# Attention blocks of a gated transformer kernel: sums by adding transfers, tokens turned by squares, and a bank of its own for a22

## The chip, the core and the metric

The kernel runs on one core of a Trainium2 chip. The metric is device time in microseconds of one launch, the median of several runs. The engines are TensorE (PE), VectorE (DVE), ScalarE (ACT), GpSimd (POOL) and SyncE (SP); SP, ACT and POOL can each issue DMA transfers.

## What is computed

Eight batches of 512 tokens of 512 features pass four layers in float32. The change touches the first:

```python
def _L0_xattn_ref(query, kv, Wq, Wg, bg, Wkv, Wo):      # H = 16 heads of 32
    q = query @ Wq.T
    gate = sigmoid(query @ Wg.T + bg)
    k, v = split(kv @ Wkv.T, 2, axis=-1)
    q, k = feature_map(q), feature_map(k)               # where(x > 0, x + 1, exp(x)), per head
    kv_summary = einsum("bhsd,bhse->bhde", k, v)
    z = 1.0 / (einsum("bhld,bhd->bhl", q, k.sum(axis=-2))[..., None] + 1e-6)
    attn = einsum("bhld,bhde->bhle", q, kv_summary) * z
    return attn * gate @ Wo.T

x = x + tanh(g_xattn[0]) * _L0_xattn_ref(layernorm(x), ctx, ...)
x = x + tanh(g_ffn[0]) * feed_forward(layernorm(x))          # 512 -> 2048 -> 512, gelu
x = x + tanh(g_xattn[1]) * masked_softmax_attention(layernorm(x), ctx)
x = x + tanh(g_ffn[1]) * grouped_experts(layernorm(x))       # routed, 8 groups
```

## The kernel before

**Blocks and products.** The work goes batch by batch (a block is one batch). Each weight product is done as seven half-size products, with sums and differences of quarters (a11, a12, a21, a22 of the tokens, b of the weights) instead of eight products of quarters. One `step(m)` is one of these seven: eight matmuls of 128x256, then `after(m, p)`, which takes the result out of a PSUM bank. A unit (`QUp`, `GUp`, `ODown` in the attention) has banks x (products 1, 6, 7, 4), w (5, 3) and z (2). Products of one bank accumulate on each other, so a reader between them must finish before the next one of that bank starts. `steps` puts the last two products of a unit (its `order` behind `head`) after the first product of the next unit, so that they fill PE there.

**The attention loop** (`for b in range(B)`) does for block b: q (`QUp`), the numerators of block b - 1 (`numerators`, `attended`), g (`GUp`), then the output unit `ODown` of block b - 1, with the denominators of b between its steps. `denominators` writes 1/z for 16 heads, each repeated over eight rows, to a DRAM tile; `spread` reads it back so that each head's row stands on 32 partitions, and `gated` multiplies it into the gate in the next block's q steps. PE, DVE and ACT follow the scheduler's order there, except where the code puts them into `in_order`; SP and POOL issue in program order.

**The preparation of block b + 1** (`prep_xa0`, through `normed`) is a generator; `some(prep)` in the loop takes its next part. It takes statistics on DVE, normalizes on ACT, and turns the tokens into features by 16 PE transposes against the identity (four tiles, L524), each tile copied from PSUM by ACT (L526). Then `token_combinations` makes the four sums S of quarters on DVE. From the second block of the feed-forward on, the tokens are turned differently: DVE transposes squares of 32x32 (L562) and 16 DMA transfers bring the squares to their partitions (L581).

**The sums onto x.** x of a block stays in SBUF. `Down.after` adds each product, scaled by the gate, onto its quarter of x with DVE (L1048), seven times per block. After the last one x is stored to the DRAM tile `between["ff0", b]`, from which the feed-forward loads it later.

**Pools.** `t2` (`temp`) holds eight buffers of 128x512 that all copies out of PSUM, feature maps and z share in turn. PSUM has four banks `ps` (transposes, numerators, denominators) and four `acc` in the attention. `over` is the one buffer for the spread denominators. A builder (`tick`, `build_first`) loads and combines the feed-forward's weights beside all this, on DVE and SP.

Of the kernel before, what the change touches and what calls it, by code (L numbers as in the profile page):

```python
# [68 lines left out]
def flamingo_kernel(  # L69
# [46 lines left out]
    bank = {"ps": ps, "xn": awork}  # L116
# [66 lines left out]
    def store_x(ph, b):  # L183

        t = xs.pop((ph, b))
        if ph == "ff1":
            for i in range(NT):
                nc.sync.dma_start(out=out[ds(b * S + i * P, P), :], in_=t[:, i, :])
        else:

            nc.scalar.dma_start(out=between[{"xa0": "ff0", "ff0": "ff1"}[ph], b], in_=t)
# [35 lines left out]
    for h in range(P // HD):  # L227
        nc.vector.memset(heads[ts(h, HD), ts(h, 8)], 1.0)
    neg_half = const.tile([P, NT], F32, tag="neg_half", name="neg_half")
# [245 lines left out]
    def normed(ph, b, tag, normed_part=lambda t: None):  # L475

        xb = xs[ph, b]
        by_products = ph == "xa0" or tag == "ff0_0"
        xnT = work.tile([P, NC, S] if ph == "xa0" else [P, NC, NT, P], F32, tag="xnT", name=f"xnT_{tag}")
# [35 lines left out]
        if by_products:  # L515

            def normed_tile(t):
                xn[t] = bank["xn"].tile([P, D], F32, tag="xn", name=f"xn_{tag}_{t}", bufs=2)
                norm(t, xn[t])

            def turn(t):
                pt = psum(f"pt_{tag}_{t}").rearrange("p (c q) -> p c q", q=P)
                for c in range(NC):
                    nc.tensor.transpose(pt[:, c, :], xn[t][:, ts(c, P)], ident)  # L524
                if ph == "xa0":
                    nc.scalar.copy(xnT[:, :, ts(t, P)], pt)  # L526
                else:
                    nc.scalar.copy(
                        xnT[:, :, t].rearrange("p q (c i) -> p c q i", c=NC),
                        pt.rearrange("p c (q i) -> p c q i", q=NC),  # L530
                    )

            if ph == "xa0" and b == 0:
                normed_tile(0)
                normed_tile(1)
                yield
                for t in range(NT):
                    turn(t)
                    if t + 2 < NT:
                        normed_tile(t + 2)  # L540
                    yield
                return xnT
            if ahead:
                normed_tile(0)
                yield
            for t in range(NT):
                if not ahead:
                    normed_tile(t)
                elif t + 1 < NT:
                    normed_tile(t + 1)  # L550
                turn(t)
                normed_part(t)
                yield
            return xnT
# [3 lines left out]
        xn = bank["xn"].tile([P, NC, NT, P], F32, tag="xn", name=f"xn_{tag}")  # L558
# [18 lines left out]
        for q in range(NC):  # L577
            for l in range(NC):
                with here("gpsimd"):
                    queue = nc.sync if tag.startswith("ff1") else nc.gpsimd  # L580
                    queue.dma_start(out=xnT[ts(l, HD), q], in_=xn[ts(q, HD), l])  # L581
# [6 lines left out]
    def features_of(ph, xnT):  # L588

        if ph == "xa0":  # L590
            return xnT.rearrange("p c (t q i) -> p c t q i", q=NC, i=HD)
        return xnT.rearrange("p q t (c i) -> p c t q i", c=NC)
# [7 lines left out]
    def keys_values():  # L600
# [15 lines left out]
        def projected(what, pair):  # L616
            p = banks[what, pair] = psum(f"p{what}_{pair}")
            for c in range(NC):
                nc.tensor.matmul(
                    p, lhsT=ctxT[pair][:, c, :], rhs=w_kv[what, c], start=c == 0, stop=c == NC - 1  # L620
                )
# [58 lines left out]
    def token_combinations(ph, b, xnT):  # L680

        s = work.tile([P, 4, 2, H2], F32, tag="S", name=f"S_{ph}_{b}", bufs=1)
        if ph == "xa0":
            v = features_of(ph, xnT).rearrange("p c t q i -> p c t (q i)")
            a11, a12, a21, a22 = (v[:, ts(h, 2), ts(r, 2)] for r in range(2) for h in range(2))
            to = s.rearrange("p k c (t i) -> p k c t i", t=2)
        else:
            a11, a12, a21, a22 = (xnT[:, :, ts(r, 2), ts(h, 2 * HD)] for r in range(2) for h in range(2))
            to = s.rearrange("p k c (q t i) -> p k (c q) t i", q=2, t=2)
        nc.vector.tensor_tensor(to[:, 0], a21, a22, ALU.add)  # L690
        nc.vector.tensor_tensor(to[:, 1], to[:, 0], a11, ALU.subtract)
        nc.vector.tensor_tensor(to[:, 2], a11, a21, ALU.subtract)
        nc.vector.tensor_tensor(to[:, 3], a12, to[:, 1], ALU.subtract)
        if ph == "xa0":
            return to.rearrange("p k c t (q i) -> p k c t q i", i=HD)
        return to.rearrange("p k q t (c i) -> p k c t q i", c=2)
# [12 lines left out]
    def cross_attention(b):  # L709
# [23 lines left out]
        for c in range(NC):  # L733
            for r in range(2):
                nc.tensor.matmul(  # L735
                    pst[ts(r, M), :],
                    lhsT=ctxT[:, c, :],
                    rhs=features_of("ff1", xnT)[:, c].rearrange("p (u r) q i -> p r u q i", r=2)[:, r],
                    start=c == 0,
                    stop=c == NC - 1,  # L740
                )
# [46 lines left out]
    def prep_ff1(b):  # L788
# [4 lines left out]
        for c in range(NC):  # L793
            for t in range(NT):
                nc.tensor.matmul(
                    plt[ts(t, E), :],
                    lhsT=router_sb[:, c, :],
                    rhs=features_of("ff1", xnT)[:, c, t],
                    start=c == 0,
                    stop=c == NC - 1,  # L800
                )
# [69 lines left out]
    class Unit:  # L871
# [3 lines left out]
        order, head = ORDER, 5  # L875

        def step(self, m):
            name = BANK[m]
            if m in OPENS:
                self.banks[name], self.numbers[name] = acc_bank(f"{name}_{self.tag}")  # L880
            self.product(m, self.banks[name])
            self.after(m, self.banks[name])
            if m in CLOSES and self.numbers[name] is not None:
                idle_banks.append(self.numbers[name])
# [5 lines left out]
        def mark(self, m, k):  # L890

            return dict(start=m in OPENS and k == 0, stop=True, skip_group_check=True)

    class Up(Unit):
# [6 lines left out]
        def product(self, m, p):  # L901
            xnT, s = blocks[self.ph, self.b][0:2]
            v = features_of(self.ph, xnT)
# [113 lines left out]
    class Down(Unit):  # L1017
# [21 lines left out]
        def after(self, m, p):  # L1039

            xb = xs[self.ph, self.b]
            parts = {1: (1, 1), 2: (1, 1), 6: (1, 2), 7: (2, 2), 4: (2, 1), 3: (1, 2)}
            todo = [(parts[m], p)] if m in parts else []
            if m == 7:
                todo.append(((2, 2), self.banks["w"]))
            for (r, c), src in todo:
                dst = xb[:, ts(r - 1, 2), ts(c - 1, H2)]
                nc.vector.scalar_tensor_tensor(dst, src, GATE[self.ph], dst, ALU.mult, ALU.add)  # L1048
# [3 lines left out]
            if m == 3:  # L1052
                stores.append((self.ph, self.b))
# [193 lines left out]
    def denominators(b, q):  # L1247
# [7 lines left out]
        nc.vector.tensor_scalar(z, pd, ATT_EPS, None, ALU.add)  # L1255
        yield
        for r in range(2):
            nc.vector.reciprocal(z[:, ts(r, H2)], z[:, ts(r, H2)])
            yield
        over[b] = dram.tile([P, S], F32, tag=f"over{b}", name=f"over_{b}")  # L1260
        nc.sync.dma_start(out=over[b], in_=z)
        yield

    def spread(b):

        rows = over[b].rearrange("(c h k) t -> c k h t", c=NC, k=8)
        over[b] = aunits.tile([P, NC, S], F32, tag="over", name=f"spread_{b}")
        for h in [slice(0, 2), slice(2, 4)] if b == B - 1 else [slice(0, 4)]:
            for c in range(NC):
                nc.sync.dma_start(out=over[b][ts(c, HD), h], in_=rows[c, 0, h].partition_broadcast(HD))  # L1270
# [41 lines left out]
    class ODown(Down):  # L1312
        def __init__(self, b):
            super().__init__("xa0", b, 2)
            self.prefix = "x"

# [42 lines left out]
    projected("k", 0)  # L1359
    projected("k", 1)  # L1360
# [34 lines left out]
    set_aside()  # L1395
    first.close()
    bank["acc"] = phase.enter_context(tc.tile_pool(name="acc", bufs=4, space=PSUM, reuse_waits="tile"))
    aunits = phase.enter_context(tc.tile_pool(name="attention_units", bufs=1, reuse_waits="tile"))
    in_order -= {"tensor", "vector", "scalar"}
# [9 lines left out]
    for b in range(B):  # L1409
# [4 lines left out]
        for n, (u, m) in enumerate(steps([q])):  # L1414
# [5 lines left out]
            if n == 4:  # L1420
                flush()
                if b < B - 1:
                    some(prep)
            tick()
        if done:
# [3 lines left out]
        for n, (u, m) in enumerate(steps([g])):  # L1429
# [12 lines left out]
            if n == 3 or n > 3 and not done:  # L1442
# [10 lines left out]
        for n, (u, m) in enumerate(steps([ODown(done[0])] if done else [])):  # L1453
# [9 lines left out]
            if n in ((0, 1, 3, 5) if b < B - 1 else (6,)):  # L1463
                some(prep)
            tick()
        for _ in prep:
            pass
# [53 lines left out]
    for u, m in [*steps([ODown(B - 1)]), *late]:  # L1521
        u.step(m)
    late.clear()
# [12 lines left out]
    bank["xn"] = hpool  # L1536
# [11 lines left out]
    def groups():  # L1548
        nc.vector.tensor_copy(mg_f, mg_i)
        for g in range(G):  # L1550
            nc.vector.tensor_scalar(of_group[:, g, :], mg_f, float(g), None, ALU.is_equal)
# [10 lines left out]
    EARLY = (25,27,29,31,33)  # L1562
# [100 lines left out]
```

## Time and profile before

| what | value |
|---|---|
| median of three runs | 2017.96 us (2016.71 to 2019.13) |
| profiled execution, its own time | 2017.31 us |
| its span (first to last instruction) | 2015.5 us |
| busy: PE, DVE, ACT, POOL | 99%, 75%, 32%, 11% of the span |
| granted TensorE clock | 0.999 |
| DMA moved | 508.81 MB, 252 GB/s on average |

In the profile a line such as `L916 PE MATMUL x_q<-xnT_xa,w_q` gives the code line, engine, operation, and the tile written and the tiles read. Line L60 is a helper through which instructions in program order pass, so tiles tell more there than lines. The attention stage lies between about 45 and 378 us of the span; the keys and values stand before it, the feed-forward layers behind it.

### The profile page before, as it was taken

The page shows a single profiled execution, that of the slowest core. Times are in us where ns is not written, and L with a number is a line of the kernel's source. Part 1 is how long each engine was busy: PE and PEld are TensorE (multiplying, and loading weights), DVE is VectorE, ACT ScalarE, POOL GpSimd, SP SyncE. Part 2 cuts the span into 40 slices and gives each one's busy share as a digit, 9 for nine tenths or more (in the row PEclk, how much of TensorE's full clock was granted, in tenths as well). Part 3 has the DMA queues.
Part 4 walks back from the last instruction along what each step waited for, and adds up shares of the span by engine and source line. Part 5 has one row for each costly group of instructions (what it writes and reads, how often), then busy time and mean ns, then how long its engine had stood idle before and what let it go on. Part 6 is the DMA issues. An engine that isn't in the chain of part 4 may idle for free.

```text
span 2015.5 us, 35095 instructions
## 1 busy us (share of the span) xinstructions
PE 1999.7 (99%) x12428; PEld 1777.3 (88%) x12428; DVE 1509.6 (75%) x3012; ACT 648.4 (32%) x1294; POOL 220.6 (11%) x387
## 2 busy tenths in 40 slices
PE   9999999999999999999999999999999999999998
PEld 5888887899989899999989889898989888898988
DVE  4788888676857676767868687877778786877758
ACT  3543443323242424233344232313132232313121
POOL 3000000101010101011211120110202020110000
PEclk9999999999999999999999999999999999999999
DMA  7366555799999998999987969696978879696865
GB/s 210 131 214 185 185 162 165 228 324 290 317 292 301 301 299 282 305 297 292 316 265 259 313 213 316 191 309 194 307 228 248 278 231 300 195 317 182 280 202 172
DMA packets 318061, 508.81 MB, mean 252 GB/s; under 512 B 42944, under 2 KB 109664, under 8 KB 313792
## 3 DMA queue, kind: packets, MB, share of 16 engines
q1 hardware_dynamic: 302768, 464.05, 72.7%
q0 software_dynamic: 9264, 19.31, 3.4%
q10 hardware_dynamic: 5856, 23.20, 3.1%
q8 instruction: 101, 1.65, 0.3%
q14 instruction: 72, 0.59, 0.1%
HBM read 413.04 MB, written 69.27 MB: 239 GB/s over the span
## 4 chain that ended last, share of the span: by engine, by line
PE 94%; DVE 4%; ACT 1%; issue 1%; DMA 0%; POOL 0%; SPq 0%; DVEq 0%; ACTq 0%
PE x_ff L916 27%; PE w_ff L916 13%; PE x_ff_down L1111 13%; PE w_ff_down L1111 9%; PE z_ff L916 7%; PE v_ff_down L1111 4%; PE z_ff_down L1111 4%; PE x_xa_down L1032 2%; PE x_q L916 2%; PE x_g L916 2%; PE w_xa_down L1032 1%; PE w_g L916 1%; PE w_q L916 1%; PE pst L735 1%; PE pv L60 1%; PE z_q L916 1%
## 5 line engine op out<-in xcount | busy, mean ns | idle before, releaser
L916 PE MATMUL w_ff<-S_ff,w_ff 128*128 128x256 f32 x1280 | 303.8, 380 | 0.2 <-DVE up_ff L1009 0.2
L916 PE MATMUL x_ff<-S_ff,w_ff 128*128 128x256 f32 x1280 | 302.9, 379 | 1.0 <-ACT u_ff L928 1.0
L916 PE MATMUL x_ff<-xnT_ff,w_ff 128*128 128x256 f32 x1280 | 297.4, 380 | 0.0
L928 ACT COPY u_ff<-x_ff 128x512 f32<-128x512 f32 x240 | 140.1, 584 | 452.7 <-PE x_ff L916 418.0
L916 PEld LDWEIGHTS x_ff<-S_ff,w_ff 128*128 128x128 f32 x1280 | 242.3, 190 | 35.0 <-ACT u_ff L928 1.6
L916 PEld LDWEIGHTS w_ff<-S_ff,w_ff 128*128 128x128 f32 x1280 | 241.0, 190 | 36.0 <-issue 2.7
L916 PEld LDWEIGHTS x_ff<-xnT_ff,w_ff 128*128 128x128 f32 x1280 | 239.5, 190 | 33.3 <-issue 1.6
L1111 PE MATMUL x_ff_down<-w_ff_down,split_ff_down 128*128 128x128 f32 x1344 | 161.9, 275 | 0.0
L1111 PEld LDWEIGHTS x_ff_down<-w_ff_down,split_ff_down 128*128 128x128 f32 x1344 | 155.9, 192 | 0.0
L916 PE MATMUL z_ff<-xnT_ff,w_ff 128*128 128x256 f32 x640 | 152.9, 380 | 0.0
L1125 DVE TENSOR_TENSOR part_ff_down<-part_ff_down 128x128 f32<-128x128 f32 x315 | 84.3, 286 | 75.6 <-ACT part_ff_down L1138 65.7
L916 PEld LDWEIGHTS z_ff<-xnT_ff,w_ff 128*128 128x128 f32 x640 | 119.9, 190 | 20.7 <-issue 5.3
L495 POOL TENSOR_TENSOR rstd_ff<-var_ff,neg_half 128x4 f32<-128x4 f32 x15 | 15.5, 1033 | 866.6 <-DVE nshift_ff L494 866.6
L1111 PE MATMUL w_ff_down<-w_ff_down,split_ff_down 128*128 128x128 f32 x896 | 107.9, 275 | 0.0
L1111 PEld LDWEIGHTS w_ff_down<-w_ff_down,split_ff_down 128*128 128x128 f32 x896 | 103.9, 192 | 0.0
L1009 DVE TENSOR_TENSOR up_ff<-w_ff,u_ff 128x512 f32<-128x512 f32 x96 | 65.6, 684 | 27.1 <-ACT u_ff L928 27.1
L976 ACT ACTIVATE a_ff<-a_ff,b_sb 128x256 f32<-128x256 f32 x128 | 58.1, 501 | 84.9 <-DVE a_ff L971 84.9
L1111 PE MATMUL x_ff_down<-w_ff_down,a_ff 128*128 128x128 f32 x672 | 82.9, 275 | 0.0
L1111 PE MATMUL w_ff_down<-w_ff_down,s_ff 128*128 128x128 f32 x672 | 82.8, 275 | 0.0
L971 DVE TENSOR_TENSOR a_ff<-w_ff,u_ff 128x512 f32<-128x512 f32 x64 | 43.9, 685 | 52.0 <-ACT u_ff L928 51.5
L999 DVE SCALAR_TENSOR_TENSOR g_ff<-th_ff,x_ff 128x512 f32<-128x512 f32 x48 | 32.7, 680 | 65.1 <-ACT th_ff L998 65.1
L1111 PEld LDWEIGHTS w_ff_down<-w_ff_down,s_ff 128*128 128x128 f32 x672 | 80.0, 192 | 0.8
(267 smaller groups left out, 3456.4 us busy)
## 6 DMA issues: line engine op xcount, KB each, us to landing
w_ff_down<-stream_ff SPq DMA_DIRECT2D x680, 256.0 KB
w_ff<-ff_up SPq DMA_DIRECT2D x560, 256.0 KB
stream_ff<-build_ff_down SPq DMA_DIRECT2D x49, 448.0 KB
x_ff<-x_ff SPq DMA_DIRECT2D x16, 1024.0 KB
share<-shares SPq DMA_DIRECT2D x64, 256.0 KB
ff_up<-build_ff_up SPq DMA_DIRECT2D x42, 256.0 KB
x_ff<-x_xa ACTq DMA_DIRECT2D x8, 1024.0 KB
x_ff<-x_ff ACTq DMA_DIRECT2D x8, 1024.0 KB
```

The source lines that it names most:

```text
L60: made = f(*args, **kw)
L495: nc.gpsimd.tensor_tensor(rstd, var, neg_half, ALU.pow)
L735: nc.tensor.matmul(pst[ts(r, M), :], lhsT=ctxT[:, c, :], rhs=features_of("ff1", xnT)[:, c].rearrange("p (u r) q i -> p r u q i", r=2)[:, r ...
L916: nc.tensor.matmul(p[:, n, :], lhsT=w[:, c, ts(n, P)], rhs=moving, **self.mark(m, 2 * n + c),)
L928: nc.scalar.copy(self.s[m], p)
L971: nc.vector.tensor_tensor(h, p, s, ALU.add)
L976: nc.scalar.activation(h[:, n, :], p[:, n, :], AF.Gelu, bias=b1_sb[:, f : f + 1])
L999: nc.vector.scalar_tensor_tensor(g, th, 1.0, p, ALU.add, ALU.mult)
L1009: nc.vector.tensor_tensor(u, p, s, ALU.add)
L1032: nc.tensor.matmul(p[:, t, :], lhsT=a[:, k, ts(t, P)], rhs=w[k // 2][:, k % 2, :], **self.mark(m, 2 * k + t),)
L1111: nc.tensor.matmul(p[bank][:, place, :], lhsT=operand[k][:, c, :], rhs=w[at // 4][:, ts(at % 4, P)], start=bank not in opened, stop=True, ...
L1125: return lambda: nc.vector.tensor_tensor(m(k), m(k), m(by), ALU.add)
```

## The change

- The output unit's products are taken in the order 1, 2, 4, 6, 5, 7, 3, all seven before the next unit (`head` 7), and product 4 opens a PSUM bank y of its own, from the pool `ps`.
- In blocks 0 to 6 each sum onto x is made of a copy by ACT, scaled by the gate, into a `t2` buffer, and a transfer of the POOL queue that adds the buffer onto `between["ff0", b]` in DRAM. There are eight such sums per block. x itself is stored to that tile before them, in the loop's q steps. The last block (7) keeps DVE's sums.
- Blocks 2 to 7 are turned by squares with 16 transfers on SP; their normalized tokens lie in the buffer `over`. Blocks 0 and 1 keep the PE transposes, with the layout of the squares.
- The denominators of blocks 0 to 6: ACT adds epsilon, one transfer writes 16 rows to DRAM, a second brings them back as 128 x 64, DVE takes the reciprocal of that, a third writes it to `over`'s DRAM tile of 16 rows. All three are on the POOL queue.
- The parts of the preparation are taken at other steps. The keys of the first two context pairs are projected with their matmuls interleaved. `groups` keeps DVE in program order.

```diff
@@ store_x @@
-        t = xs.pop((ph, b))
+        t = xs[ph, b] if ph == "xa0" else xs.pop((ph, b))
...
@@ normed @@
-        by_products = ph == "xa0" or tag == "ff0_0"
-        xnT = work.tile([P, NC, S] if ph == "xa0" else [P, NC, NT, P], F32, tag="xnT", name=f"xnT_{tag}")
+        by_products = tag in ("xa0_0", "xa0_1", "ff0_0")
+        xnT = work.tile([P, NC, NT, P], F32, tag="xnT", name=f"xnT_{tag}")
...
-        xn = bank["xn"].tile([P, NC, NT, P], F32, tag="xn", name=f"xn_{tag}")
+        xn = bank["xn"].tile([P, NC, NT, P], F32, tag=bank["tag"], name=f"xn_{tag}")
...
-                    queue = nc.sync if tag.startswith("ff1") else nc.gpsimd
+                    queue = nc.sync if ph == "xa0" or tag.startswith("ff1") else nc.gpsimd
...
@@ projected @@
-        def projected(what, pair):
-            p = banks[what, pair] = psum(f"p{what}_{pair}")
+        def projected(what, *pairs):
+            for pair in pairs:
+                banks[what, pair] = psum(f"p{what}_{pair}")
             for c in range(NC):
-                nc.tensor.matmul(
-                    p, lhsT=ctxT[pair][:, c, :], rhs=w_kv[what, c], start=c == 0, stop=c == NC - 1
-                )
+                for pair in pairs:
+                    nc.tensor.matmul(
...
@@ Unit.step @@
-            name = BANK[m]
-            if m in OPENS:
-                self.banks[name], self.numbers[name] = acc_bank(f"{name}_{self.tag}")
+            name = self.bank_of[m]
+            if m in self.opens:
+                if name == "y":
+                    self.banks[name], self.numbers[name] = halves(psum(f"{name}_{self.tag}")), None
+                else:
+                    self.banks[name], self.numbers[name] = acc_bank(f"{name}_{self.tag}")
...
@@ Down.after @@
+            if 4 in self.opens and m == 5:
+                todo.append(((2, 2), p))
+            if 4 in self.opens and m == 7:
+                todo[1:] = [((2, 1), p)]
             for (r, c), src in todo:
-                dst = xb[:, ts(r - 1, 2), ts(c - 1, H2)]
-                nc.vector.scalar_tensor_tensor(dst, src, GATE[self.ph], dst, ALU.mult, ALU.add)
+                if self.b == B - 1:
+                    dst = xs[self.ph, self.b][:, ts(r - 1, 2), ts(c - 1, H2)]
+                    nc.vector.scalar_tensor_tensor(dst, src, GATE[self.ph], dst, ALU.mult, ALU.add)
+                    continue
+                t = halves(temp(f"sum{m}{r}{c}_{self.tag}"))
+                nc.scalar.activation(t, src, AF.Identity, scale=GATE[self.ph])
+                nc.gpsimd.dma_start(
+                    out=between["ff0", self.b][:, ts(r - 1, 2), ts(c - 1, H2)], in_=t, accum_op=ALU.add
+                )
...
@@ denominators @@
+        of_heads = z.rearrange("(n k) t -> n k t", k=8)[:, 0, :]
+        over[b] = dram.tile([P // 8, S], F32, tag=f"over{b}", name=f"over_{b}")
+        if b == B - 1:
...
+        nc.scalar.activation(z, pd, AF.Identity, bias=eps, scale=1.0)
+        under = dram.tile([P // 8, S], F32, tag=f"under{b}", name=f"under_{b}")
+        narrow = small.tile([P, S // 8], F32, tag="narrow", name=f"narrow_{b}")
+        with here("gpsimd"):
+            nc.gpsimd.dma_start(out=under, in_=of_heads)
+            nc.gpsimd.dma_start(out=narrow, in_=under.rearrange("n (u q) -> (n u) q", u=8))
+        yield
+        yield
+        nc.vector.reciprocal(narrow, narrow)
+        with here("gpsimd"):
+            nc.gpsimd.dma_start(out=over[b].rearrange("n (u q) -> (n u) q", u=8), in_=narrow)
...
@@ ODown @@
+            self.order, self.head = (1, 2, 4, 6, 5, 7, 3), 7
+            self.bank_of, self.opens = {**BANK, 4: "y"}, (*OPENS, 4)
...
@@ the attention loop @@
-    projected("k", 0)
-    projected("k", 1)
+    projected("k", 0, 1)
...
+    stores.append(("xa0", 0))
+    flush()
...
+    bank.update(xn=aunits, tag="over")
...
-            if n == 4:
-                flush()
-                if b < B - 1:
-                    some(prep)
+            if n == 4 and b + 1 < B - 1:
+                stores.append(("xa0", b + 1))
+            if n in ((4,) if b == 0 else (0, 3, 5) if b < B - 1 else ()):
+                some(prep)
             tick()
+        flush()
...
-            if n == 3 or n > 3 and not done:
+            if n in ((0, 2) if b < B - 1 else (3,)) or n > 2 and not done:
                 some(prep)
...
-            if n in ((0, 1, 3, 5) if b < B - 1 else (6,)):
+            if n in ((2,) if b < B - 1 else (6,)):
                 some(prep)
+            if n == 4 and b < B - 1:
+                for _ in prep:
+                    pass
             tick()
-        for _ in prep:
-            pass
+        while b < B - 1 or prep not in ready:
+            if next(prep, prep) in (prep, "last"):
+                ready.add(prep)
+                if b == B - 1:
+                    break
+                for _ in prep:
+                    pass
+                break
...
@@ behind the loop @@
-    for u, m in [*steps([ODown(B - 1)]), *late]:
+    for n, (u, m) in enumerate([*steps([ODown(B - 1)]), *late]):
         u.step(m)
+        if n == 4:
+            for _ in prep:
+                pass
```

## The prediction

> **What bounds the kernel now.** First the head of the page:
>
> ```profile
> span 2015.5 us, 35095 instructions
> ...
> PE 1999.7 (99%) x12428; PEld 1777.3 (88%) x12428; DVE 1509.6 (75%) x3012; ACT 648.4 (32%) x1294; POOL 220.6 (11%) x387
> ```
>
> TensorE is busy in 99% of the span, so only two things can move the time: PE work that disappears, and PE waits that come or go. The change lies in the attention stage (about 45 to 378 us), so next the busy time of one whole block there, from one block's numerators to the next:
>
> ```profile
> core 0: us, PE busy (x) PEld busy (x) DVE busy (x) ACT busy (x) POOL busy (x), PEclk, DMA share, GB/s
> 205.20:245.60 40.40, 40.40 (x225) 33.70 (x224) 32.45 (x54) 17.34 (x31) 1.70 (x2) 1.00 0.52 171
> ```
>
> PE has no gap in it, DVE is at 80%, ACT at 43%, the DMA engines at half. What PE does in it shows in its timeline (start, length, line):
>
> ```profile
> 221.27 0.66 PE L524 MATMUL pt_xa<-ident,xn_xa 128*128 128x128 f32 x4
> 221.76 1.89 PE L916 MATMUL x_g<-xnT_xa,w_g 128*128 128x256 f32 x8
> 223.49 0.60 PE L524 MATMUL pt_xa<-ident,xn_xa 128*128 128x128 f32 x4
> 223.93 1.89 PE L916 MATMUL w_g<-S_xa,w_g 128*128 128x256 f32 x8
> 225.66 1.89 PE L1032 MATMUL z_xa_down<-w_o,a 128*128 128x256 f32 x8
> 227.38 0.60 PE L524 MATMUL pt_xa<-ident,xn_xa 128*128 128x128 f32 x4
> 227.82 1.89 PE L1032 MATMUL x_xa_down<-w_o,s_xa 128*128 128x256 f32 x8
> ```
>
> The distance from start to start counts, not the length: a product of eight matmuls holds the queue 1.73 us (223.93 to 225.66), a turned tile 0.44 to 0.49 us. That is the price of a turn, because PE takes them in order and idles nowhere near them. Last, all that PE waits for:
>
> ```profile
> PE x_g L916 <- ACT u_g L928: 1.8, 3, 1.2
> PE pk L60 <- DMA w_k<-in_wkv: 1.1, 1, 1.1
> ...
> PE pd L60 <- DVE q L673: 1.1, 1, 1.1
> ...
> PE x_xa_down L1032 <- DVE x_xa L1048: 0.8, 1, 0.8
> ```
>
> With the rows of 0.7 and 0.6 us that follow, the attention's own waits (without the keys' 1.1) come to 5.0 us, and all of them have a late ACT or DVE behind them.
>
> **Part 1, the turns.** Blocks 2 to 7 lose four turned tiles each. In the block shown they cost 0.49 + 0.44 + 0.44 + 0.43 = 1.80 us, six blocks 10.8 us. All of it is on the path. The group's mean of 277 ns would give 96 x 0.277 = 27 us, but it counts overlapped ends; I take the pace. (The Trainium skill, "TensorE: Matmul & The Clock Gate", Part 4: PE-mode transpose, has about 275 ns for a transpose within one kernel, which is this mean; as a cost it would make the gain an estimated 26 us. No gap in this trace supports that.)
>
> In their place come four squares on DVE (the same instruction at L562: median 702 ns, 2.8 us a block) and 16 transfers of 64 KB, now on SP. SP issues the same transfers in the second feed-forward at 0.59 us (L581), so 9.4 us of SP per block, where SP spends some 22 of 43 us between 202 and 245 us. Squares end near the third step of g; the next block's first product is 13 steps, 22 us, later; 9.4 + 2 of landing need 11.5. Behind an ff_up store (7 issues, 13.1 us at 204.8) they would be 2 to 3 us late. There are four such stores: 0 to 10 us in all.
>
> **Part 2, the sums.** DVE loses seven L1048 per block (0.747 us: 5.2), two reciprocals of 256 columns (3.4) and the add of epsilon (0.7); with squares 2.8 and a reciprocal of 64 columns (a quarter of 1.73: 0.4) it falls by 6.1 to about 26 of 38.6 us. ACT gains eight gated copies and one z at about 0.59 (L928 reads a bank so) and loses four turn copies (0.58): plus 3, to 20 of 38.6. Neither becomes the bound. The bank waits get looser: a sum's reader has at least one other product (1.73 us) before its bank is written again, also because a22 has a bank of its own. Of the 5 us of old waits I take half as gone: 2.5 (none to all).
>
> Each copy needs a buffer of the eight of t2 until its adding transfer has read it. Step by step the buffer's next user comes six products or more later, 10 us. No adding transfer is in the trace. Bounds: below, a plain 64 KB transfer of the POOL queue; above, twice the bytes.
>
> ```profile
> xnT_xa<-xn_xa POOLq DMA_DIRECT2D x128, 64.0 KB, 6.4
> ...
> xnT_ff<-xn_ff POOLq DMA_DIRECT2D x112, 64.0 KB, 5.1
> ...
> ctxd<-in_ctx POOLq DMA_DIRECT2D x16, 128.0 KB, 4.0
> ```
>
> 5 us, or 10 if the old value must be fetched as well: just inside the cover. Two sums for one quarter must follow each other: m=7 behind m=5 on (2,2), one product apart, holds the POOL queue some 3.5 us; behind it stand only the last two sums. Seven stream_ff pieces of one DRAM tile are issued back to back, so sums to different quarters should not wait for each other. DMA load: the stage's share is about 0.57 of 325 us, 185 us; 6 MB of squares and 14.7 MB of sums at 282 GB/s (queue q0: 19.31 MB in 3.4% of the span) add 21 and 52, doubled for the adds 104: 258 to 310 of 314 us. Full at the worst, not over.
>
> **Part 3, the denominators.** Here a wait grows. Before, in the block shown:
>
> ```profile
> 221.41 0.69 DVE L1255 TENSOR_SCALAR z<-pd 128x512 f32<-128x512 f32 x1 [0.28 <-PE pd L60]
> 222.13 3.37 DVE L1258 RECIPROCAL z<-z 128x256 f32<-128x256 f32 x2
> ...
> 241.23 1.28 DVE L1275 SCALAR_TENSOR_TENSOR th<-th,spread 128x512 f32<-128x512 f32 x2
> ```
>
> ```profile
> 225.53 0.32 SPq L60 DMA_DIRECT2D over<-z  x1
> 227.53 1.74 SPq L60 DMA_DIRECT2D spread<-over  x4
> ```
>
> The row goes out at 225.5, lands in 2.0, and the spread moves its 1 MB at about 150 GB/s until 235; its reader runs at 241.2. Now three POOL transfers of t each stand in the chain, two of them with POOL waiting: 222.5 (z on ACT) + 3t + 0.5 + 7.5. The reader stands ten products after 221.8, at 239.1, so it is late by 3t - 8.6. Behind it in DVE's queue stand q's features and the (2,2) part, which PE needs before q's last product writes its bank, five products (8.6 us) later; that DVE work takes 4.7, so 3.9 us are covered. PE loses 3t - 12.5 per block: nothing up to t = 4.2. The rows give 1.9 (fastest square) to 7.7; these are 16 KB in a half-idle stage, so I take 3.5: hidden.
>
> (Against the move speaks the Trainium skill, "SBUF — State Buffer", Summary: rules for kernel authors: hide a DMA under VectorE by SP's or ACT's queue, because GpSimd's descriptors starve while VectorE is in a two-port mode. It gives 620 ns alone and 3100 beside a copy; by that t would be an estimated 6 and the loss 5.5 a block. In the trace, POOL issued 112 squares at 0.50 us each beside a busy DVE, so I do not add it.)
>
> **Part 4, the rest.** Keys of two pairs interleaved: while PE waits 1.1 us for the second w_k piece, the other pair's first product (0.9) runs: 0.9 gained. The store of x moves ahead, one ACT issue (0.35 us) as before. The last block keeps DVE's sums; the smaller edits (index views, groups) cost nothing beside a full PE.
>
> **Sum.** New waits from late squares, late spreads and full buffers: 0 to 10, I take 3. The profiled execution took 2017.3 us (span 2015.5 and 1.8 around it; median of the runs 2018.0, 0.03% more). 2017.3 - 10.8 - 0.9 - 2.5 + 3.0 = 2006.1.
>
> **Rivals.**
> - *The chain of the denominators outlasts its cover* (slower). Place: DVE waits at L1275 for the spread, PE for q's bank. It decides from t = 4.2 and cancels the gain near t = 5.1 (2.8 us x 6 blocks = 17). At t = 5.5: 4.0 x 6 = 24 instead of 3: 2027. For it: the POOL rows of 5.1 and 6.4. Against: those are bursts of 16 in fuller stages, and ctxd with eight times the bytes has 4.0.
> - *The DMA engines fill up.* If an add costs double, the stage's share goes from 0.57 to nearly 1, and squares and weights come late in turn; the gain is used up at about 14 us of waits: 2017.
> - *All old waits go.* DVE's 6 us less per block end the late u_g and q, and nothing new comes: 2017.3 - 10.8 - 0.9 - 5 = 2000.6, with restarts 1999.5.
>
> **How the numbers follow.** Forecast (2003 to 2012) 0.51; old waits all gone 0.13; DMA full 0.13; chain too long 0.23. About 0.2%, 4 us, is what a measurement of this kernel can tell from no change. Faster 0.64, same 0.13, slower 0.23. The range goes from all gains, 1999, to the chain at t near 5.4, 2025; the forecast's own range is 2000 to 2013.
>
> **What would show it.** Right: L524 falls from 112 and 16 to 32 for pt_xa in all; a block's period falls from 40.4 to about 38.6; PE's waits stay near 5 us; L1275 waits at most a few us; spread follows z by about 12 us. Wrong: PE waiting for DVE q parts or ACT u copies (buffers of t2 held by transfers), for xnT or S in blocks 2 to 7, a landing time of the small POOL transfers over 4.2 us, or DMA share near 1 between 50 and 370 us.

## The result and the profile after

The changed kernel takes 2090.69 us (median of six runs, 2084.49 to 2092.97) against 2018.55 for the kernel before beside it (six runs, 2016.71 to 2021.66): ratio 1.0356, 95% interval 1.0344 to 1.0369. Slower by 72 us, where 12 us less was forecast, and outside the range. The profiled execution took 2089.23 us. The head of its page, and the line of the software queue q0, which stood at 19.31 MB and 3.4% before:

```profile
span 2087.5 us, 35330 instructions
...
PE 2016.9 (97%) x12332; PEld 1779.7 (85%) x12332; DVE 1471.2 (70%) x2975; ACT 674.5 (32%) x1333; POOL 296.8 (14%) x464
...
q0 software_dynamic: 25168, 34.69, 8.3%
```

The 96 turns are gone (PE has 12332 matmuls instead of 12428), and PE is nonetheless busy for longer in a span of which it fills only 97%. Where the time went is read from two starts, q's first product and the feed-forward's first: 44.78 and 377.74 us before, 55.03 and 449.43 after. So 10.3 us were lost ahead of the attention and 61.4 in it (394.4 instead of 333.0); the feed-forward behind takes 1638.1 instead of 1637.8. The windows of the attention, of the kernel after:

```profile
core 0: us, PE busy (x) PEld busy (x) DVE busy (x) ACT busy (x) POOL busy (x), PEclk, DMA share, GB/s
...
150.00:200.00 50.00, 44.31 (x220) 35.42 (x219) 27.63 (x50) 22.57 (x39) 12.82 (x13) 0.93 0.88 223
200.00:250.00 50.00, 41.89 (x209) 33.87 (x208) 32.38 (x56) 20.62 (x36) 12.79 (x13) 0.90 0.82 200
250.00:300.00 50.00, 44.56 (x218) 34.62 (x218) 25.17 (x45) 20.71 (x37) 12.81 (x13) 0.97 0.81 200
300.00:350.00 50.00, 39.09 (x185) 28.96 (x184) 24.98 (x43) 17.82 (x32) 12.79 (x13) 0.91 0.89 224
```

Before, a block's window had PE at 40.40 of 40.40, clock 1.00 and DMA share 0.52. In these windows of the kernel after PE stands 5 to 11 of 50 us, the granted clock falls to 0.90, and the DMA engines are at 0.81 to 0.89 on average. What is waited for (waiter, releaser: total us, times, longest), for PE, DVE, ACT and POOL in this order:

```profile
PE w_q L923 <- DVE qs_q L1234: 27.7, 5, 7.4
PE x_q L923 <- DMA xnT_xa<-xn_xa: 8.1, 1, 8.1
PE pk L60 <- ACT xnT_xa L60: 7.2, 1, 7.2
...
DVE qs_q L1234 <- DMA x_ff<-sum_xa_down: 28.6, 5, 9.8
DVE narrow L1291 <- DMA narrow<-under: 15.6, 5, 3.6
DVE th L1308 <- DMA spread<-over: 0.8, 1, 0.8
...
ACT fe_q L681 <- DMA x_ff<-sum_xa_down: 46.3, 5, 11.4
ACT u_q L935 <- DMA x_ff<-sum_xa_down: 16.8, 7, 5.4
...
POOL x_ff L60 <- DMA x_ff<-sum_xa_down: 57.6, 6, 12.9
POOL narrow L60 <- DMA under<-z: 22.6, 7, 4.8
```

PE waits for DVE, and DVE and ACT wait for adding transfers: neither qs_q nor fe_q nor u_q reads what such a transfer writes. They write `t2` buffers that the transfer has yet to read. L1308 (L1275 before), where the prediction looked for the denominators, waits 0.8 us. Landing times (after the KB of one: median us from issue to landing):

```profile
x_ff<-sum_xa_down POOLq DMA_DIRECT2D x56, 256.0 KB, 7.7
...
under<-z POOLq DMA_DIRECT2D x7, 32.0 KB, 4.2
narrow<-under POOLq DMA_DIRECT2D x7, 32.0 KB, 2.1
over<-narrow POOLq DMA_DIRECT2D x7, 32.0 KB, 2.0
```

The add lands in 7.7 us, between the prediction's bounds of 5 and 10. But a buffer is held from ACT's copy on, not from the issue. One block, ACT and POOL:

```profile
209.87 0.55 POOL L60 DMA_DIRECT2D under<-z  x1 [1.56 <-ACT z L1283]
214.25 0.69 ACT L1062 ACTIVATE sum_xa_down<-z_xa_down,gates_half 128x512 f32<-128x512 f32 x1 [2.32 <-PE z_xa_down L1039]
214.81 0.60 POOL L60 DMA_DIRECT2D narrow<-under  x1 [4.38 <-DMA under<-z]
...
218.03 0.55 POOL L60 DMA_DIRECT2D over<-narrow  x1 [2.63 <-DVE narrow L1291]
...
218.57 4.98 POOL L60 DMA_DIRECT2D x_ff<-sum_xa_down  x4
219.92 1.26 ACT L1062 ACTIVATE sum_xa_down<-x_xa_down,gates_half 128x512 f32<-128x512 f32 x2 [1.10 <-PE x_xa_down L1039]
...
229.77 3.65 POOL L60 DMA_DIRECT2D x_ff<-sum_xa_down  x3 [6.22 <-DMA x_ff<-sum_xa_down]
```

The copy of 214.25 is ready at 214.9 and is sent at 218.6, because POOL stands 4.38 and 2.63 us in the denominators' chain; with the median landing its buffer is free at about 226, 12 us after the copy began. The copies of 219.92 are sent behind a wait of 6.22 us for the earlier sum of the same quarter, at 229.8 and later: free at about 238, 18 us after they began. Each issue also takes 1.25 us of POOL (4.98 for four).

### The profile page after: what moved, and what is told of

It is laid out like the page before. It is cut to its first block, busy times and chain, and to the rows that moved or that the text cites. A ratio compares the mean times of both kernels' runs of the same rounds, so it can differ in the third digit from the quotient of the medians.

```text
span 2087.5 us, 35330 instructions
## 1 busy us (share of the span) xinstructions
PE 2016.9 (97%) x12332; PEld 1779.7 (85%) x12332; DVE 1471.2 (70%) x2975; ACT 674.5 (32%) x1333; POOL 296.8 (14%) x464
## 3 DMA queue, kind: packets, MB, share of 16 engines
q0 software_dynamic: 25168, 34.69, 8.3%
## 4 chain that ended last, share of the span: by engine, by line
PE 81%; DMA 7%; issue 7%; DVE 2%; POOL 2%; SPq 1%; ACT 1%; DVEq 0%; POOLq 0%; ACTq 0%
PE x_ff L923 26%; PE w_ff L923 13%; PE x_ff_down L1128 13%; PE w_ff_down L1128 8%; PE z_ff L923 7%; PE v_ff_down L1128 4%; PE z_ff_down L1128 4%; DMA x_ff<-sum_xa_down 4%; SPq L60 1%; POOL x_ff L60 1%; DMA under<-z 1%; PE pst L738 1%; PE pr L783 1%; PE x_q L923 1%; DMA x_xa<-in_x 0%
## 5 line engine op out<-in xcount | busy, mean ns | idle before, releaser
L923 PEld LDWEIGHTS w_ff<-S_ff,w_ff 128*128 128x128 f32 x1280 | 241.0, 190 | 35.7 <-issue 2.7
L60 POOL DMA_DIRECT2D x_ff<-sum_xa_down x56 | 69.0, 1754 | 191.7 <-ACT sum_xa_down L1062 128.6
L60 POOL DMA_DIRECT2D xnT_xa<-xn_xa x128 | 63.1, 498 | 131.3 <-PE x_ff L923 56.2
```

Source lines behind the costliest of these rows:

```text
L60: made = f(*args, **kw)
L923: nc.tensor.matmul(p[:, n, :], lhsT=w[:, c, ts(n, P)], rhs=moving, **self.mark(m, 2 * n + c),)
```

## Experiments

Two theories: **buffers** (the `t2` buffers are held too long, and DVE and ACT, behind them PE, wait for them) and **load** (the adding transfers fill the DMA engines, and everything else that moves comes late). A rival to both is the denominators' chain. Ratios are to the kernel before on the same chip, which had medians of 2017.1 to 2017.4.

| kernel | us | ratio and 95% interval |
|---|---|---|
| e1, adds, early store in order | 2073.35 | 1.0274 (1.0239 to 1.0308) |
| e2, e1 with buffers of their own | 2045.67 | 1.0138 (1.0122 to 1.0153) |
| e4, e1 with plain transfers | 2022.71 | 1.0025 (1.0014 to 1.0037) |
| e5, e4 without second writes | 2027.90 | 1.0049 (1.0023 to 1.0074) |
| e6, e1 with the old denominators | 2050.81 | 1.0166 (1.0145 to 1.0186) |
| e3, sums by DVE | 2021.32 | 1.0019 (1.0008 to 1.0030) |
| e11, e3 and adds that nobody reads | 2050.43 | 1.0164 (1.0144 to 1.0184) |
| e9, e3 with earlier preparation | 2014.75 | 0.9989 (0.9980 to 0.9999) |
| e9d, e9 with the old denominators | 2026.83 | 1.0053 (1.0036 to 1.0070) |
| e10, e9 with turns by PE | 2034.61 | 1.0088 (1.0074 to 1.0102) |
| e13, e9 with the old output unit | 2020.98 | 1.0023 (1.0014 to 1.0032) |
| e17, e9 with denominators together | 2018.29 | 1.0007 (0.9998 to 1.0016) |

**The store of x.** In the kernel after, the store of block 1's x stands early in ACT's queue, in front of the work on keys and values:

```profile
37.72 0.38 ACTq L191 DMA_DIRECT2D x_ff<-x_xa  x1
38.15 1.07 ACT L60 COPY xnT_xa<-pt_xa 128x512 f32<-128x512 f32 x2 [14.93 <-DMA x_xa<-in_x]
```

ACT stood 14.9 us for the load of the x that this store sends. e1 keeps that store in ACT's program order:

```diff
-            nc.scalar.dma_start(out=between[...][ph, b], in_=t)
+            with here(*(["scalar"] if ph == "xa0" else [])):
+                nc.scalar.dma_start(out=between[...][ph, b], in_=t)
```

> Keeps the whole change; only the early store of x is kept in program order on ACT, so that it stands behind the first q products and not before the turn copies of block 0. The changed kernel's ACT stood 14.9 us there for the load of block 1, and its first q product started 10.3 us later than before. Buffer theory (t2 held by the adding transfers): 2089 - 10 = 2079, the attention's waits stay. Rivals (denominators' chain too long; DMA engines full): the same 2079. If nothing moves, the start was not this store.

2073.35: 17 us less than after (the interval of this ratio leaves 7 us to either side). q begins at 43.77 instead of 55.03. The 17 us are more than the 10 expected, though the interval just takes 10 in: the edit keeps the later blocks' stores in order too, and ACT's wait of 4.9 us for another load of x, at about 260 us in the kernel after, is gone as well. The attention stays long, 387.0 us, with the same waits:

```profile
DVE qs_q L1235 <- DMA x_ff<-sum_xa_down: 32.2, 5, 10.9
...
ACT fe_q L682 <- DMA x_ff<-sum_xa_down: 41.7, 5, 11.1
```

**Buffers of their own.** e2 is e1, with the copies in five buffers that nothing else uses. The room comes from the fourth x buffer, which is dropped.

```diff
-                t = halves(temp(f"sum{m}{r}{c}_{self.tag}"))
+                t = halves(aunits.tile([P, 512], F32, tag="sum", ..., bufs=5))
```

> Adding transfers as in e1, but the gated copies take five buffers of their own instead of the eight they share with z, th and q's features (the room comes from the extra x tile of every fourth block, which is dropped). Buffers held: the waits of DVE qs_q and ACT fe_q for an earlier adding transfer (19 to 42 us in e1) go, and the time falls from 2073 to about 2050, what the load of the transfers alone cost in e11. Load alone: the waits only change their name (a gated copy waits for the add five products earlier), and the time stays within 5 us of 2073.

2045.67, 28 us below e1. The waits of qs_q and fe_q for transfers are gone. What is left stands with the copies themselves, which now wait for the five buffers, and with the squares' transfers, and the DMA engines are no emptier than in the kernel after. So 28 us is what these five buffers save, not necessarily all that the holding costs. The waits, and one window:

```profile
PE x_q L922 <- DMA xnT_xa<-xn_xa: 12.7, 2, 8.8
```

```profile
ACT sum_xa_down L1061 <- DMA x_ff<-sum_xa_down: 20.6, 8, 5.1
```

```profile
200.00:250.00 50.00, 40.32 (x195) 31.30 (x194) 31.33 (x58) 20.10 (x35) 12.78 (x13) 0.90 0.91 228
```

**What of a transfer costs.** e4 writes instead of adding (the sums are left out), from the same buffers with the same waits in the code. e5 sends the second write of a quarter, which waits for the first, to a tile that nobody reads.

```diff
-                    out=between["ff0", self.b][...], in_=t, accum_op=ALU.add
+                    out=between["ff0", self.b][...], in_=t
```

> As e1, but the 56 transfers of the sums write instead of add (same queue, bytes and waits; the sums themselves are left out, only the last write of a quarter remains). If the adding itself is slow in the DMA engines (104 us of engine time for 14.7 MB in the changed kernel), landing falls from 7.7 us to about 5 and the waits shrink in proportion: buffer theory 2040 to 2055. DMA engines full: 2015 to 2030. Denominators' chain: 2075.

> As e4, and the second write of each quarter goes to another DRAM tile, so that no transfer of a sum waits for an earlier one (the sums are left out as in e4). Buffer theory: POOL's waits of 9 to 13 us per block for the earlier sum go, buffers come free about 10 us sooner: 10 to 25 us below e4, to 2020 to 2035. DMA engines full: the same as e4, since the bytes are the same. Denominators' chain: 2075.

e4 takes 2022.71, within 2 us of e3, which makes the sums on DVE. In its profile q0 and the landing read:

```profile
q0 software_dynamic: 14416, 34.69, 5.8%
...
x_ff<-sum_xa_down POOLq DMA_DIRECT2D x56, 256.0 KB, 4.2
```

The same 14.7 MB in 45 us of the 16 engines' time (5.8% of 2024.1 less the 3.6% of 2019.6 that e3's q0 has), 329 GB/s; as adds in e1 it is 99 us (8.3% of 2068.9 less the same), 148 GB/s, and 272 packets for a transfer instead of 80 ((25168 - 9936)/56 and (14416 - 9936)/56). The adding itself costs 50 us in e1, not the way over DRAM. e5 missed: 5 us above e4 instead of below. Its two waits of PE ahead of q are longer (6.0 and 4.9 us instead of 3.9 and 3.1); why is open. With a landing of 4.2 us the waits for the earlier write, 23.2 us of POOL in e4, cost no time that their removal gives back. In company with adds they were not tried alone.

**The load alone.** e3 gives all blocks DVE's sums and stores x after them. e11 is e3 with 56 adds that touch no buffer of `t2`: they add a weight tile onto a tile in DRAM that nobody reads, which a second store of x (7 MB more) fills first.

```diff
+                if self.b < B - 1:
+                    nc.gpsimd.dma_start(out=aside[self.b][...], in_=w_o[0], accum_op=ALU.add)
```

> Undoes the sums alone: DVE adds all sums onto x in SBUF again and x is stored behind the last one; squares, denominators' chain, bank y and the new order stay. Buffer theory: DVE's and ACT's waits for adding transfers vanish and with them most PE waits: 2005 to 2015. Chain of the denominators as the cause: the waits stay, 2060 to 2080. DMA engines full: 2010 to 2025, since 15 MB of adds go, but with squares still landing late here and there.

> As e3 (DVE adds onto x in SBUF), and beside it the same 56 adding transfers of 256 KB on the POOL queue, now from a fixed weight tile onto a DRAM tile that nobody reads (with a second store of x to that tile): the DMA load and the POOL queue's waits of the adds, and no buffer of t2 held. Buffer theory (ACT and DVE wait for t2 buffers that adds hold): 2020 to 2035, close to e3. DMA theory (the adds fill the 16 engines and squares, spreads and weights come late): 2055 to 2080, close to e1.

e3 2021.32, e11 2050.43, between the two ranges expected: the load costs 29 us, at most, since the second store and the adds' time in POOL's queue are in it. One window of 50 us, and two of 5 us around a wait of PE for squares (4.5 us, until 217.3):

```profile
200.00:250.00 50.00, 43.26 (x213) 33.48 (x212) 38.99 (x70) 16.30 (x30) 12.80 (x13) 0.97 0.96 252
...
210.00:215.00 5.00, 2.52 (x11) 1.55 (x9) 4.86 (x9) 0.00 (x0) 1.39 (x2) 1.00 1.15 191
215.00:220.00 5.00, 2.69 (x8) 2.19 (x9) 4.56 (x12) 0.00 (x0) 2.41 (x4) 0.78 1.13 333
```

The share adds up packet times and can pass 1. So the mean over 50 us hides stretches in which the DMA engines are full, here around a wait of PE.

So both theories hold. From e1 to e3, 52 us: about 28 with the buffers (e1 less e2), about 24 with the load and what is left of the holding (e2 less e3; e11 has 29).

**The denominators.** e6 is e1, e9d is e9, each with the old denominators (`if True:` in the place of `if b == B - 1:`, so DVE takes the reciprocals of 128x512 in every block).

> As e1 (all sums by adding transfers), with the denominators as in the kernel before: reciprocals on DVE, one transfer on SP, none on the POOL queue. Measured so far: e1 2073, sums by DVE 2021, plain transfers 2023. If the slow adds are what counts, and the chain only adds a wait in front of them on the POOL queue, 2055 to 2075. If chain and adds need each other (adds queue up behind the chain and are issued in one burst), 2025 to 2045. The prediction's slower rival (chain too long by itself) is contradicted already by e3, and would say under 2030.

> As e9, with the denominators as in the kernel before (two reciprocals of 1.7 us on DVE, one transfer on SP). If the chain of three transfers costs by the wait of DVE for it: 3 to 8 us below e9. If its cover holds (prediction: hidden), the 3 us of DVE per block come back: 0 to 4 us above e9.

The chain gains 12 us with DVE's sums (2026.83 against 2014.75, three times the most that was expected: without it DVE is late in emptying a bank, and PE waits 8.6 us for x_xa at L1059). Together with adds it loses 23 (2073.35 against 2050.81, between the two ranges expected). The largest total of waits for adds in e6, ACT fe_q, is 29.7 us instead of 41.7, DVE qs_q 19.1 instead of 32.2. That fits the POOL queue, where three of the chain's steps no longer stand between the sums; the runs don't separate it from the buffer that z takes.

**Preparation.** With the output unit's `head` 7, q has only five steps from block 2 on. So step 5 in `(0, 3, 5)` doesn't come, and what was to be asked for there goes out one call later. e9 is e3 with

```diff
-            if n in ((4,) if b == 0 else (0, 3, 5) if b < B - 1 else ()):
+            if n in ((4,) if b == 0 else (0, 2, 4) if b < B - 1 else ()):
```

> As e3, with the preparation's parts taken at steps 0, 2, 4 of q rather than 0, 3, 5: from block 2 on q has five steps there, so that step 5 never came and the last squares ran a part later. In e3 one block's period was 47.6 us instead of 39, with PE waiting for S and S for the squares' transfers. If late squares are what is left of the cost, 2008 to 2014. If the rest is DVE's waits for the denominators' chain, 2018 to 2022, as e3.

2014.75, 6.6 below e3 and the fastest here: 0.1% under the kernel before, with an interval that just leaves out 1, but less than the 0.2% that the prediction took for no change. In e3 one block stood out:

```profile
PE x_q L923 <- DVE S_xa L696: 3.3, 1, 3.3
```

Its period was 47.57 us, in e9 all lie between 39.3 and 40.9, and this wait is 0.4. The squares of that block go out 20.1 us behind the numerators in e3 (162.02 to 182.12) and 17.0 in e9 (164.56 to 181.59).

**The other parts, each undone in e9.** e10 turns by PE in all blocks (`by_products = ph == "xa0" or tag == "ff0_0"`). e13 takes out the two lines with the output unit's order, head and bank y. e17 issues the four denominator matmuls together and two steps later.

> e9 with x turned by TensorE in blocks 2 to 7 too, as before the change: nothing else differs. The prediction's pace (1.80 us of TensorE a block, nothing of it hidden): six blocks, 10.8 us, so 2014.8 + 10.8 = about 2025.5. Rival, the pt group's mean of 277 ns is the price: 96 x 0.277 = 27, so about 2041. Rival, the squares bring as much waiting as the turns cost: 2013 to 2018.

> e9 with the output unit's order, head and banks as before the change (no bank of its own for a22, seven steps of q beside it). If the looser banks removed about half of the old 5 us of waits, as the prediction had it, this one is 2 to 4 us slower than e9: 2017 to 2019. If the bank is worth nothing with DVE making the sums: 2013.5 to 2016.

> e9 with the four denominator matmuls two steps later and kept together. In e9 most blocks issue them in two pairs of about 1.0 us each, while four at a time take 1.0 us in all, since they use different quarters of the array. Theory: six blocks save about 1.0 us each, 2008 to 2010. Rival: the chain of the denominators starts 3.5 us later, th waits for the spread at L1308 and TensorE for q's bank behind it: 2015 or more.

e10: 2034.61, 20 us above e9, neither 10.8 nor 27. A quiet block of its PE timeline prices the turn as the prediction did, by the distance to the next start: 0.49, 0.43, 0.44 and 0.58, 1.94 us in all.

```profile
222.21 0.66 PE L533 MATMUL pt_xa<-ident,xn_xa 128*128 128x128 f32 x4
222.70 1.89 PE L923 MATMUL x_q<-xnT_xa,w_q 128*128 128x256 f32 x8
...
226.16 0.60 PE L533 MATMUL pt_xa<-ident,xn_xa 128*128 128x128 f32 x4
226.59 1.89 PE L923 MATMUL z_g<-xnT_xa,w_g 128*128 128x256 f32 x8
```

Six blocks make 11.6. PE idles 14.4 us in the attention instead of 6.9 (for xn_xa 5.7 instead of 1.4, for u_q 3.4 instead of 0.6). And in five blocks the numerators behind a turn hold PE for 1.81 us (218.34 to 220.15) instead of 1.07, 3.7 in all, while the denominator matmuls, in two pairs in e9, stand together again and give back about 5. These terms add up to about 18 of the 20. e13: 2020.98, 6.2 above e9 where 2 to 4 was expected, with PE waiting for its old banks:

```profile
PE x_xa_down L1039 <- DVE x_xa L1059: 6.3, 8, 1.1
```

In e9 that row is 0.4. e17: 2018.29, where 2008 to 2010 was the theory. The rival's number came, its mechanism didn't: DVE's wait for the spread (L1310 here) is 0.4 us in all, and five waits of 0.9 to 1.0 us are new:

```profile
PE z_xa_down L1039 <- ACT th L1260: 4.8, 5, 1.0
```

In e9 the second pair of denominator matmuls (0.99 us) stands just ahead of z_xa_down and covers this wait. Kept together, they save their microsecond and PE idles for it; single waits of 1.3 to 1.4 us for qs_q, x_xa and z come on top.

## Why the prediction was wrong, point by point

The step that failed is part 2, the price of a held buffer; in the sum it stood within the 3 us (0 to 10) for new waits. The cover of "10 us" was compared with the transfer's own 5 or 10, "just inside the cover". The landing was sized rightly, 7.7 us, but the time in POOL's queue ahead of the issue was left out: 4.4 and 2.6 us for the denominators' chain, 6.2 for an earlier sum, 1.25 for each issue. In the block shown buffers were held an estimated 12 to 18 us. The prediction had named the parts of this: the transfers of the chain "two of them with POOL waiting" (costed for the chain alone) and the hold of "some 3.5 us" behind which "stand only the last two sums" (two do stand behind the held one, but the hold is 6.2). It never added them to the buffer's time, although PE waiting for buffers "held by transfers" is among its signs of being wrong. Buffers alone: 28 us by e2.

- **The rival "the DMA engines fill up"** had its mechanism right and its size too small. The bound of the doubled add, 104 us of engine time, is the measured one, 99. "Full at the worst, not over" was taken as nearly harmless, 14 us of waits to use up the gain; the load costs 24 to 29, though the share averages 0.81 to 0.99 over windows of 50 us. An average under 1 says little: around PE's waits e11 has 1.13 and 1.15.
- **The store of x, costed at nothing** as one ACT issue: 17 us. Its issue is cheap, but it waits for its x to load and ACT's queue stood behind it. The wait of a moved instruction, and what is queued behind it, was not asked for in this place.
- **The slow rival, the chain of the denominators**, was refuted with its place and its price: the three landings make 8.3 us, under the 10.5 taken, and L1308 waits 0.8 us. (The transfers are of 32 KB, not 16, so that ctxd has four times the bytes and not eight.) Without adds the chain gains 12 us, with them it loses 23, not through the spread; through POOL's queue or z's buffer, the runs don't say. The landings are 4.2, 2.1 and 2.0 us beside a DVE at 50 to 65%, and 1.9, 2.1 and 2.0 in e9, without adds. The Trainium skill, "SBUF — State Buffer", Summary: rules for kernel authors, speaks of GpSimd's descriptors starving while VectorE is in its 2x or 4x mode; these landings show no such loss, but no run shows the mode.
- **Part 1, the turns.** The price was right, 1.94 a block in e10 against 1.80. What they cost in e10 is larger, 20 us, by waits and by slower numerators that the turns bring. The squares, costed at 0 to 10 us of waits, cost 8.1 in one wait of the kernel after, and 0.4 in e9, without adds and asked for one call earlier; that a call would fall away with `head` was not seen, 6.6 us. SP needed 10 to 13.6 us for a block's 16 issues, not 9.4.
- **Old waits, half of 5 us gone.** Too low for the output unit, worth 6.2 by e13. But with sums by DVE others come: from q's first product to the feed-forward's PE idles 6.9 us in e9 against 5.2 before, and the denominator matmuls stand in two pairs, about 1 us more in each of five blocks. So the forecast's 2006 wasn't reached without adds either: 2014.75.
- **Part 4, the interleaved keys**, taken at 0.9: q begins at 43.35 in e3, 43.77 in e1 and 44.62 in e9, 0.2 to 1.4 us before the 44.78 of the kernel before.
- **The clock was not in the sum at all.** Once PE waits for long, the next products are slow (kernel after):

```profile
219.66 1.89 PE L1039 MATMUL w_xa_down<-w_o,s_xa 128*128 128x256 f32 x8
229.66 3.75 PE L923 MATMUL x_q<-xnT_xa,w_q 128*128 128x256 f32 x8 [8.11 <-DMA xnT_xa<-xn_xa]
233.20 2.78 PE L923 MATMUL z_q<-xnT_xa,w_q 128*128 128x256 f32 x8
235.82 1.89 PE L923 MATMUL x_q<-S_xa,w_q 128*128 128x256 f32 x8
```

From start to start 3.54 and 2.62 us instead of 1.73: a wait of 8.1 us cost 10.8. The granted clock (next to the DMA share) is half there, and whole 5 us later:

```profile
230.00:235.00 5.00, 5.00 (x13) 3.88 (x13) 2.23 (x4) 0.58 (x1) 4.68 (x5) 0.50 0.91 190
235.00:240.00 5.00, 5.00 (x25) 4.41 (x24) 1.09 (x2) 1.74 (x3) 0.00 (x0) 1.00 1.17 233
```

The Trainium skill, "TensorE: Matmul & The Clock Gate", Part 1: The HAM clock gate, has half the clock after an idle window of about 3.4 us, until about 3.4 us of work; by that figure the loss would be an estimated 1.7 us. The trace shows 2.7 here. Over the whole attention, the kernel after and then e9:

```profile
55.03:449.43 394.40, 342.17 (x1696) 269.88 (x1697) 228.66 (x400) 164.71 (x288) 93.96 (x97) 0.94 0.75 188
```

```profile
44.62:376.06 331.44, 324.57 (x1697) 259.86 (x1698) 261.94 (x456) 128.59 (x232) 25.03 (x41) 1.00 0.63 189
```

PE idles 52.2 us instead of 6.9, and takes 17.6 us more for as many matmuls, which goes with the lower clock.

The account of the 72 us, in the order of the experiments: 2090.7, less 17 for the early store (e1), less 28 for the buffers (e2), less 24 for the load (e3), less 7 for the preparation (e9), is 2014.75. Another order would divide the middle terms differently, as e6 shows. From e1 to e3 the attention shortens by 47.9 us, 35.7 of them idle time of PE (47.9 to 12.2) and 12.1 busy time for the same 1697 matmuls. What stays open: how this divides between the 28 and the 24, how much of the load's 24 to 29 is time in POOL's queue and how much the DMA engines, and why the scheduler put that store so early.

## What to carry to other kernels

A transfer that takes over an engine's work holds its buffer from the moment it is written until the transfer has landed, and all that stands ahead of it on the issuing queue counts: sum that, not the landing time alone, and compare it with the buffer's next writer. A part can be a gain by itself and a loss in company (the denominators' chain: 12 won with DVE's sums, 23 lost beside adds on the same queue), so undo the parts one by one before a change is kept or dropped whole. An instruction that is moved takes its waits along; ask of each what it waits for at the new place.

## What the runs showed of the hardware

- An adding transfer of 256 KB into DRAM (e1) took 2.2 times the DMA engine time of a plain one (e4; 148 against 329 GB/s), 272 packets instead of 80, and 7.5 us to land instead of 4.2. Its issue took 1.25 us of POOL in the kernel after, 0.73 as a plain one in e4; the chain's small transfers take 0.55.
- An average DMA share under 1 can hide full stretches: from 100 us on e11 has 0.88 to 0.99 over windows of 50 us but 1.13 and 1.15 over 5 us around a wait of PE, and with these transfers, whose results nobody reads, the kernel took 29 us more.
- Long waits of TensorE cost more than their length: in the kernel after 10.8 us for 8.1, and in e3 a wait of 3.3 us was followed by a product of 3.46 us (202.56 to 206.02) instead of 1.73.
